# Softplus of a selective scan in two ScalarE operations instead of three

## The chip, the core and the metric

The kernel runs on one core of one Trainium2 chip. The metric is the device time of one execution in microseconds, of which the median of three runs is taken. All data are float32.

## What is computed

Two layers follow each other on an input of 8 images of 64 x 64 places and 192 channels. The first is a Mamba-2 block with depthwise convolutions and a small MLP; the change doesn't touch it. The second is a selective scan (SS2D) in four directions, and its core is this, cut from the reference:

```python
x_dbl = jnp.einsum('bkdl,kcd->bkcl', xs, x_proj_weight)
dts, Bmat, Cmat = ...                       # 12, 16 and 16 rows
dts = jnp.einsum('bkrl,kdr->bkdl', dts, dt_projs_weight)
delta = jax.nn.softplus(dts + dt_projs_bias[None, :, :, None])
A = -jnp.exp(A_logs).reshape(K, D_INNER, D_STATE)      # K = 4, D_INNER = 384, D_STATE = 16
def step(hst, inp):
    d, bm, cm, uu = inp
    dA = jnp.exp(d[..., None] * A[None])
    dBu = (d * uu)[..., None] * bm[:, :, None, :]
    hst = dA * hst + dBu
    y = jnp.einsum('bkdn,bkn->bkd', hst, cm)
    return (hst, y)
```

Softplus is log(1 + exp(v)), here of v = dts + bias, with a bias drawn between -4 and -2.

## The kernel before, in words

The first layer runs for the first 5 ms, then the second layer takes the images one after the other. For each image there is a stage of projections and convolutions (`front`), then the scan (`main`), then normalisation, gate and output projection (`finish`). The `finish` of an image, the `front` of the next and the beginning of its scan (`prologue`, `prologue_of`) share one stage. In that stage a planner, `Flow.run`, writes out the order on each engine: each `step(engine, cost, ...)` carries a cost in microseconds, a change of ScalarE's function table costs 1.3 in its plan, and of all chains' next steps the one that can start first by these costs is put next. The order is then fixed on every engine. A table is loaded where the set changes (`"explog"` for Exp and Ln, `"silu"` for Silu), and once more ahead of `main`. There are nine such stages: the first has no `finish`, the last no `front`, and seven have both.

`main` is written out by hand, and each engine works through its instructions in program order. An image has 32 steps: four directions k, and for each 8 tiles of 512 places. A step has 24 units u = 3 p + d: p counts 8 pairs of states, d counts 3 blocks of 128 channels. One unit does the following.

- DVE runs two scans over 128 x 512 (L1596): `hs` = `ea` x state + `g`.
- POOL copies the last state (`cy`, L1608) and multiplies `hs` by the C row (`hc`, L1610).
- ACT computes `ea` = exp(A delta) for the unit two ahead, two operations (L1569; three buffers), and then two or three `pw` = (delta u) times B (L1554) for units further on. Their numbers are 3, 3 and 2 for d = 0, 1 and 2.
- PE turns `pw` into `g` for the next unit by eight transposes (L1580; two buffers) and then adds `hc` of the unit before into `y` (L1625). For the first direction it also adds a skip term.
- DVE adds a finished `y` into `yacc` after the last p (three times a step, in the last unit and the first two of the next step).

Between the units stand the pieces which prepare the next step, one list for each unit number (`prepare`). Per d they are: `step` (PE, `p_dt`, L1468), `soft` (ACT, three operations, L1475 to L1477), `delta` (DVE, L1482), `times_u` (POOL, `du`, L1489), `turn` (PE, `p_du`, L1495), `keep_du` (DVE, `duT`, L1502), and `repeat_delta` (four DMAs on SP, `dr`, L1536). `p_d`, `p_b`, `p_dt` and `p_du` all share one PSUM bank there, so that each waits until the one before has been read. The list, cut to what matters:

```python
7: [(keep_b,), (step, 0)],
8: [(soft, 0)],
9: [(delta, 0), (step, 1)],
10: [(soft, 1), (times_u, 0)],
11: [(delta, 1), (turn, 0), (repeat_delta, s, 0)],
12: [(keep_du, 0), (step, 2), (times_u, 1)],
13: [(soft, 2)],
14: [(delta, 2), (turn, 1)],
15: [(keep_du, 1), (times_u, 2)],
```

The last step of an image prepares nothing, so 8 x 31 = 248 steps are prepared inside a loop and 8 in the stages between the images.

Of the kernel before, what the change touches and what calls it, by code (L numbers as in the profile page):

```python
# [9 lines left out]
AF = mybir.ActivationFunctionType  # L10
ALU = mybir.AluOpType
# [18 lines left out]
NP1 = N // 2  # L30

EXPLN = "natural_log_exp_and_others"


_P96 = [("cw1", 18), ("cb1", 2), ("l1w", 2), ("l1b", 2), ("cw2", 18), ("cb2", 2), ("l2w", 2), ("l2b", 2), ("fb2", 2)]
# [20 lines left out]
def explog(tc):  # L56

    tc.keep_in_program_order(tc.nc.scalar.preload_act_table_set(EXPLN))

# [31 lines left out]
class Flow:  # L91
# [24 lines left out]
    def pool(self, tag, n):  # L116
        self.slots[tag] = [0.0] * n
# [34 lines left out]
    def run(self):  # L152
        while self.chains:
# [10 lines left out]
            elif req[0] != "wait":  # L164
                engine, weight, do, _, table = req
                if table and table != self.table:
                    self.table = table
                    if table == "explog":
                        self.keep(self.tc.nc.scalar.preload_act_table_set(EXPLN))
                for ins in do() or ():  # L170
# [11 lines left out]
def step(engine, weight, do, after=None, table=None):  # L182
    return engine, weight, do, after, table
# [846 lines left out]
def layer1(tc, consts, x1s, mv1, out, w_in, w_x, w_dt, w_out):  # L1030
    nc = tc.nc
# [6 lines left out]
    with ExitStack() as ctx:  # L1038
        pool = lambda name, bufs, **kw: ctx.enter_context(tc.tile_pool(name=name, bufs=bufs, **kw))
        wp = pool("w1", 1)  # L1040
        sp = pool("s1", 1)
# [49 lines left out]
        o = lambda ins: keeper[-1](ins)  # L1091
# [309 lines left out]
        def scan(xo):  # L1401
# [5 lines left out]
            pools, ready = {}, {}  # L1407
# [12 lines left out]
            def prepare(s, bank=lambda name: mp.tile([128, TT], F32, name=name, tag="mm")):  # L1420
# [3 lines left out]
                st = state[s]  # L1424
# [47 lines left out]

                def soft(d):
                    st["sp", d] = a = pools["pr1"].tile([128, TT], F32, name="spa", tag="tmp")
                    o(nc.scalar.activation(a, st["p_dt", d], AF.Abs))  # L1475
                    o(nc.scalar.activation(a, a, AF.Exp, scale=-1.0))
                    o(nc.scalar.activation(a, a, AF.Ln, bias=1.0))  # L1477

                def delta(d):
                    st["de", d] = pools["pr1"].tile([128, TT], F32, name="de", bufs=3)  # L1480
                    o(
                        nc.vector.scalar_tensor_tensor(  # L1482
                            st["de", d], st["p_dt", d], 0.0, st["sp", d], ALU.max, ALU.add
                        )
                    )

# [13 lines left out]
                def keep_du(d):  # L1500
# [13 lines left out]
                    6: [(turn_b,)],  # L1514
# [9 lines that stand above are left out]
                    16: [(turn, 2)],  # L1524
# [5 lines left out]
            def repeat_delta(s, d):  # L1530

                state[s]["dr", d] = dr = pools["dr1"].tile([128, 2, TT], F32, name="dr")
                de = state[s]["de", d]
                for f in range(2):
                    for i in range(2):
                        o(nc.sync.dma_start(out=dr[i * 64 : i * 64 + 64, f], in_=de[f * 64 : f * 64 + 64]))  # L1536
# [135 lines left out]
            def prologue_of(f, d):  # L1672

                yield "wait", "xd"
                yield "take", "mm"
                yield step("PE", 0.95, lambda: ready["step"](d))
                yield "take", "tmp"
                yield step("ACT", 1.9, lambda: ready["soft"](d), None, "explog")
                r = yield step("DVE", 0.7, lambda: ready["delta"](d))
                f.give("mm", r)  # L1680
                f.give("tmp", r)
                yield step("SP", 0.1, lambda: repeat_delta(0, d), r)
                yield "take", "tmp"
                r = yield step("POOL", 1.3, lambda: ready["times_u"](d), r)
                yield "take", "mm"
                r = yield step("PE", 0.6, lambda: ready["turn"](d))
                f.give("tmp", r)
                yield "wait", "bt"
                r = yield step("DVE", 0.7, lambda: ready["keep_du"](d))
                f.give("mm", r)  # L1690
                f.at["du", d] = r
# [32 lines left out]
            def chains(f, mq, front_pools):  # L1724
                f.pool("tmp", 2)
                return [prologue(f, mq, front_pools)] + [prologue_of(f, d) for d in range(DT)]
# [128 lines left out]
```

## Time and profile before

| what | value |
|---|---|
| median of 3 runs | 24186.39 us (24181.09 to 24191.97) |
| the profiled execution: its time, its span | 24176.65 us, 24174.9 us |
| first layer and first `front`, until the first scan | 5049 us |
| one image's scan loop (second image: 7456.4 to 9620.4) | 2164 us |
| from the last scan of an image to the first of the next | 238 to 240 us |
| ACT ea L1569, pw L1554 | 709 and 601 ns each, 8123.2 and 8875.8 us in all |
| ACT softplus L1475, L1476, L1477 | 575, 630 and 630 ns, 768 of each |
| DVE scan L1596, POOL hc L1610 | 1263 and 2373 ns each |

A profile line names the source line, the engine, the operation, the tile written and those read, the shape and the count; then the busy time, the mean duration, and the time that the engine stood idle just before, with what ended it (`<-`). Back-to-back operations of one engine overlap a little, so the distance from start to start can be smaller than a duration. In a timeline the columns are start, length, engine, line; a bracket gives the idle time before. With 24 units and 31 of 32 steps alike, one step of about 67.6 us (first direction 68.5 us) repeats through the loops.

### The profile page before, as it was taken

What the parts mean: (1) busy time and instruction counts of PE and PEld (TensorE: products, weight loads), DVE (VectorE), ACT (ScalarE), POOL (GpSimd) and SP (SyncE); (2) the same over time, 40 slices, a digit from 0 to 9 for tenths busy, and PEclk for the clock granted to TensorE, in tenths of its full rate; (3) what the DMA queues carried; (4) which work ended last, traced back from release to release, by engine and by line L of the source; (5) the groups of instructions that cost most, each with busy time, mean ns of one, the idle gap of its engine ahead of it and who ended that gap; (6) DMA issues with size and microseconds to landing.
All of it is one profiled execution on the core that took longest, in us unless ns stands there. A gap on an engine that the chain in (4) does not pass through costs nothing.

```text
span 24174.9 us, 313055 instructions
## 1 busy us (share of the span) xinstructions
PE 20986.5 (87%) x100036; PEld 10182.8 (42%) x100036; DVE 21386.3 (88%) x22093; ACT 21415.5 (89%) x38076; POOL 16907.4 (70%) x13639
## 2 busy tenths in 40 slices
PE   7999999978888888888888888888888888888888
PEld 4444444434443444344434443444344434443444
DVE  7888888779998998899889988998899989998998
ACT  5666766679998999899989998999899989998998
POOL 1111111159986998699869986998699779977997
PEclk8999999989999999999999999999999999999999
DMA  2111111122222222222222222222222222222222
GB/s 49 44 44 44 49 44 42 36 86 67 68 66 87 68 67 68 89 66 66 69 87 68 68 68 86 67 68 70 84 68 67 76 78 67 68 75 82 67 67 58
DMA packets 1129702, 1608.05 MB, mean 67 GB/s; under 512 B 259360, under 2 KB 458432, under 8 KB 1118848
## 3 DMA queue, kind: packets, MB, share of 16 engines
q1 hardware_dynamic: 1128064, 1588.03, 23.4%
q8 instruction: 806, 13.21, 0.2%
q14 instruction: 832, 6.82, 0.1%
HBM read 1024.65 MB, written 160.17 MB: 49 GB/s over the span
## 4 chain that ended last, share of the span: by engine, by line
POOL 53%; PE 25%; issue 8%; DVE 6%; ACT 5%; DMA 2%; SPq 1%; POOLq 0%; DVEq 0%; ACTq 0%
POOL hc L1610 47%; POOL cy L1608 4%; PE y L1625 3%; PE p_f L953 3%; DVE xs L1200 3%; PE p_f L973 2%; PE p_x L445 2%; PE g L1580 2%; ACT pw L1554 2%; DMA xc<-xo 2%; PE p_o L870 1%; POOL du L1489 1%; ACT ea L1569 1%; PE p_y L787 1%; PE p_d L1439 1%
## 5 line engine op out<-in xcount | busy, mean ns | idle before, releaser
L1610 POOL TENSOR_TENSOR hc<-hs,cb 128x1024 f32<-128x1024 f32 x6144 | 14577.7, 2373 | 10.3 <-POOL cy L1608 6.7
L1596 DVE TENSOR_TENSOR_SCAN hs<-ea,cy,g 128x512 f32<-128x512 f32 x10752 | 13069.7, 1263 | 783.2 <-PE g L1580 468.3
L1554 ACT ACTIVATE pw<-duT,bt 128x384 f32<-128x384 f32 x16384 | 8875.8, 601 | 11.6 <-DVE duT L1502 11.6
L1625 PE MATMUL y<-hc,sel 128*64 128x512 f32 x24576 | 6658.3, 620 | 2229.1 <-POOL hc L1610 2221.3
L1569 ACT ACTIVATE ea<-dr,an 128x512 f32<-128x512 f32 x12288 | 8123.2, 709 | 159.9 <-DVE hs L1596 131.9
L1580 PEld LDWEIGHTS g<-ident,pw 128*128 128x128 f32 x49152 | 5309.6, 141 | 4320.1 <-issue 2676.5
L1580 PE MATMUL g<-ident,pw 128*128 128x128 f32 x49152 | 6793.2, 280 | 32.4 <-DVE hs L1596 12.9
L1625 PEld LDWEIGHTS y<-hc,sel 128*64 128x64 f32 x24576 | 1229.6, 135 | 3648.1 <-POOL hc L1610 3385.1
L1489 POOL TENSOR_TENSOR du<-de,xc 128x512 f32<-128x512 f32 x768 | 982.9, 1280 | 1632.9 <-DVE de L1482 1618.2
L1608 POOL COPY cy<-hs 128x2 f32<-128x2 f32 x6144 | 1161.7, 189 | 1324.4 <-DVE hs L1596 1211.9
L1596 DVE TENSOR_TENSOR_SCAN hs<-ea,g 128x512 f32<-128x512 f32 x1536 | 1777.0, 1204 | 178.7 <-PE g L1580 138.3
L362 POOL TENSOR_TENSOR s<-xs 96x512 f32<-96x512 f32 x64 | 121.0, 1891 | 2033.2 <-DVE xs L340 1522.3
L1200 DVE SCALAR_TENSOR_TENSOR xs<-pad,p,xs 128x4096 f32<-128x4096 f32 x192 | 860.8, 4484 | 37.6 <-ACT xs L1190 30.4
L1468 PE MATMUL p_dt<-xdbl,wd 13*128 13x512 f32 x1536 | 856.8, 639 | 41.7 <-DVE de L1482 39.7
L362 POOL TENSOR_TENSOR s<-sq 96x512 f32<-96x512 f32 x128 | 210.3, 1643 | 961.7 <-ACT sq L375 890.7
L1439 PE MATMUL p_d<-xc,wx 128*44 128x512 f32 x1536 | 792.2, 598 | 95.0 <-DMA xc<-xo 95.0
L340 DVE SCALAR_TENSOR_TENSOR x<-xx,p,x 96x512 f32<-96x512 f32 x1024 | 784.4, 814 | 19.4 <-ACT x L329 19.4
L953 PE MATMUL p_f<-h,wf 96*128 96x512 f32 x1536 | 764.1, 633 | 24.4 <-ACT zs L547 14.0
L340 DVE SCALAR_TENSOR_TENSOR xs<-xin,p,xs 96x512 f32<-96x512 f32 x1024 | 749.5, 768 | 4.6 <-ACT xs L329 4.6
L1482 DVE SCALAR_TENSOR_TENSOR de<-p_dt,spa 128x512 f32<-128x512 f32 x768 | 524.1, 682 | 254.0 <-ACT spa L1477 253.0
L973 PE MATMUL p_f<-m,wf 128*96 128x512 f32 x1536 | 693.3, 602 | 0.0
L1495 PEld LDWEIGHTS p_du<-ident,du 128*128 128x128 f32 x3072 | 323.1, 141 | 743.2 <-POOL du L1489 500.3
(201 smaller groups left out, 19729.0 us busy)
## 6 DMA issues: line engine op xcount, KB each, us to landing
cb<-cd SPq DMA_DIRECT2D x4096, 128.0 KB
dr<-de SPq DMA_DIRECT2D x3072, 128.0 KB
xc<-xo SPq DMA_DIRECT2D x256, 768.0 KB
e<-csd SPq DMA_DIRECT2D x256, 384.0 KB
xl<-x SPq DMA_DIRECT2D x256, 384.0 KB
xo<-xs SPq DMA_DIRECT2D x48, 1024.0 KB
xo<-xt SPq DMA_DIRECT2D x24, 2048.0 KB
xl<-in_x SPq DMA_DIRECT2D x64, 384.0 KB
```

What stands on the lines that cost most here:

```text
L340: nc.vector.scalar_tensor_tensor(im(out[:, ct]), tap(ct, j), w[:, ct, j : j + 1], im(out[:, ct]), ALU.mult, ALU.add)
L953: nc.tensor.matmul(ps, wf1[:, ct, mt * 128 : mt * 128 + 128], h[:, ct], start=ct == 0, stop=ct == 1)
L973: nc.tensor.matmul(ps[:CP], wf2[:, kt, ct * CP : ct * CP + CP], m[:, kt], start=kt == 0, stop=kt == 5)
L1200: nc.vector.scalar_tensor_tensor(xs, tap(j), kw[:, d, j : j + 1], xs, ALU.mult, ALU.add)
L1489: o(nc.gpsimd.tensor_mul(st["du", d], st["de", d], st["xc"][:, d]))
L1554: nc.scalar.activation(st["pw", p, j][:, :, i], st["duT"][:, j].rearrange("p (g c) -> p g c", c=64), AF.Copy, scale=st["bt"][:, j, n : n + 1],
L1569: nc.scalar.activation(ea[:, f], state[s]["dr", d][:, f], AF.Exp, scale=an[:, k, p, at : at + 1])
L1580: nc.tensor.transpose(g[:, f, j * 128 : j * 128 + 128], state[s]["pw", p, j][:, 2 * d + f].rearrange("p a b -> p (a b)"), ident,)
L1596: nc.vector.tensor_tensor_scan(rev(h[:, f]), rev(ea[:, f]), rev(g[:, f]), 0.0 if first(s) else state[s - 1]["cy"][:, p, d, f : f + 1], ALU ...
L1608: o(nc.gpsimd.tensor_copy(st["cy"][:, p, d], h[:, :, last]))
L1610: o(nc.gpsimd.tensor_mul(hc, h, bc(st["cb", p], 1, [128, 2, TT])))
L1625: o(nc.tensor.matmul(y[half[f]], sel, hc[:, f], start=p == 0 and k > 0, stop=p == NP1 - 1))
```

## The change

`soft` drops the absolute value: ScalarE now computes exp(v) from PSUM, and log(1 + that). `delta` took max(v, 0) and added log(1 + exp(-|v|)); now it takes the minimum of log(1 + exp(v)) and 60 and then the maximum of that and v, so that an overflowing exp can't get through. It is still one `scalar_tensor_tensor` on VectorE, with its two tensors exchanged: the first is now the one in SBUF, the second the one in PSUM. The planner's cost for `soft` in the stages between images goes from 1.9 to 1.3. The counts of all other instructions stay, but for one table load fewer in each of the seven stages that have both `finish` and `front`.

```diff
+BIG = 60.0
...
                 def soft(d):
                     st["sp", d] = a = pools["pr1"].tile([128, TT], F32, name="spa", tag="tmp")
-                    o(nc.scalar.activation(a, st["p_dt", d], AF.Abs))
-                    o(nc.scalar.activation(a, a, AF.Exp, scale=-1.0))
+                    o(nc.scalar.activation(a, st["p_dt", d], AF.Exp))
                     o(nc.scalar.activation(a, a, AF.Ln, bias=1.0))
...
                         nc.vector.scalar_tensor_tensor(
-                            st["de", d], st["p_dt", d], 0.0, st["sp", d], ALU.max, ALU.add
+                            st["de", d], st["sp", d], BIG, st["p_dt", d], ALU.min, ALU.max
                         )
...
-                yield step("ACT", 1.9, lambda: ready["soft"](d), None, "explog")
+                yield step("ACT", 1.3, lambda: ready["soft"](d), None, "explog")
```

In the built program the change of cost moves the order in those seven stages. On ScalarE, after the three softplus and the last `yrs`, the order was: table load, one z, three yacc, ten pw, five z, table load, four ea, table load. It becomes: two yacc, ten pw, one yacc, four ea, table load, six z, table load. On PE the two matmuls of one `p_z` move from ahead of two groups of `p_o` to behind `p_du`. On SP four `dr` transfers come ahead of one `xl` load. On DVE the three deltas come ahead of the three `duT` copies in the first stage (of the first image).

## The prediction

> **What bounds the kernel now.** I read the page first: busy shares, the chain that ended last, the costliest groups.
>
> ```profile
> PE 20986.5 (87%) x100036; PEld 10182.8 (42%) x100036; DVE 21386.3 (88%) x22093; ACT 21415.5 (89%) x38076; POOL 16907.4 (70%) x13639
> ...
> POOL 53%; PE 25%; issue 8%; DVE 6%; ACT 5%; DMA 2%; SPq 1%; POOLq 0%; DVEq 0%; ACTq 0%
> ...
> L1610 POOL TENSOR_TENSOR hc<-hs,cb 128x1024 f32<-128x1024 f32 x6144 | 14577.7, 2373 | 10.3 <-POOL cy L1608 6.7
> ```
>
> Three engines are near 88%, and ScalarE (ACT), the one that the change relieves, is the busiest. But it holds only 5% of the chain; GpSimd (POOL) holds 53%, nearly all in hc. Next I cut the second image's scan loop out, by windows:
>
> ```profile
> 7457.00:9620.00 2163.00, 1865.89 (x10159) 913.88 (x10157) 2017.84 (x1877) 2137.90 (x3848) 2017.87 (x1627) 1.00 0.24 66
> ```
>
> Columns: length, then busy PE, PEld, DVE, ACT, POOL. ACT is busy 98.8% of the loop, POOL and DVE 93.3%. Busy is not bound: the question is who waits for ACT. The page's groups answer it in total, and the lines of the softplus name the waiter:
>
> ```profile
> L1482 DVE SCALAR_TENSOR_TENSOR de<-p_dt,spa 128x512 f32<-128x512 f32 x768 | 524.1, 682 | 254.0 <-ACT spa L1477 253.0
> ```
>
> So VectorE (DVE) lost 253.0 us in front of delta because softplus was late. I sorted the trace's records of L1482 by their place: per step the first delta (piece 9) waits 0, the second (piece 11) 0.51 us on average, the third (piece 14) 0.37. Over the 248 steps that are prepared inside a loop that is 126.5 and 92.9 us; some 33 us are in the eight stages between images. Last, the timeline around one third delta:
>
> ```profile
> 8852.77 2.39 POOL L1610 TENSOR_TENSOR hc<-hs,cb 128x1024 f32<-128x1024 f32 x1
> ...
> 8853.76 1.12 PE L1468 MATMUL p_dt<-xdbl,wd 13*128 13x512 f32 x2
> ...
> 8854.81 1.09 PE L1580 MATMUL g<-ident,pw 128*128 128x128 f32 x8
> 8855.09 1.30 POOL L1489 TENSOR_TENSOR du<-de,xc 128x512 f32<-128x512 f32 x1
> ...
> 8856.04 2.45 DVE L1596 TENSOR_TENSOR_SCAN hs<-ea,cy,g 128x512 f32<-128x512 f32 x2 [0.72 <-ACT pw L1554]
> ...
> 8857.53 0.63 ACT L1476 ACTIVATE spa<-spa 128x512 f32<-128x512 f32 x1
> 8858.19 0.63 ACT L1477 ACTIVATE spa<-spa 128x512 f32<-128x512 f32 x1
> ...
> 8858.86 0.69 DVE L1482 SCALAR_TENSOR_TENSOR de<-p_dt,spa 128x512 f32<-128x512 f32 x1 [0.37 <-ACT spa L1477]
> ...
> 8861.97 0.18 POOL L1608 COPY cy<-hs 128x2 f32<-128x2 f32 x1 [0.67 <-DVE hs L1596]
> ```
>
> The reader is to see three things. POOL has no idle mark until 8861.97, where it waits 0.67 us for the scan behind the delayed delta. The scan at 8856.04 is put down to ACT pw, but PE decides it: a y matmul needs hc, p_dt runs to 8854.88, g to 8855.90, then the scan starts. So of the three softplus of a step only the last is on the path.
>
> **What the Trainium skill says.** "ScalarE: Activation LUTs", What ACT_TABLE_LOAD costs: one element per cycle and lane whatever the function, and back-to-back ACTIVATEs overlap by about 93 ns. The trace agrees: Exp and Ln from SBUF take 630 ns each, Abs from PSUM 575, and pw of 601 ns starts every 507 ns. Same page, Table sets: abs is filler in every set, and natural_log_exp_and_others holds Exp and Ln; so neither removing Abs nor the new pair adds a load inside the loop, where the trace has none. "VectorE: DVE Perf Modes", Why PSUM operands drop a tier: fp32 with a PSUM operand runs at 1x; so delta with its operands exchanged should keep its cost. No run shows that order; I take 691 ns, the median of L1482.
>
> **The change, part by part.**
>
> Removed: 768 Abs. One soft takes 8856.93 to 8858.73 = 1.80 us from its start to the next instruction's. After, Exp reads PSUM (I take Abs's 0.60 from start to start; by the SBUF Exp at most 0.66) and Ln takes 0.54 until the next one starts, so 1.14. ACT is 0.66 us less per softplus, 1.98 per step, 507 us in all. This is the gain only if ACT were the bound.
>
> On the path, in the loop. Third delta: its wait goes, 0.37 per step. What would be late next is the scan before it, ending 8858.49: delta can start about there. The scan after it ends 0.37 earlier, and the 0.67 idle of POOL shrinks to 0.30. p_dt for it was there at 8854.88, ACT would come to it at 8856.93 - 2 x 0.66 = 8855.61, so PE isn't late. The sum over the 248 steps is the 92.9 us above.
>
> Second delta: its 126.5 us go as a wait but are worth nothing, because POOL runs du and hc without a gap from there until the third delta, and PE (y after hc, p_dt, g) sets scan 14. If that cover were gone, they would count: 126.5 is kept as the far end. First delta: 0. The rest of POOL's idle per step (about 4.3 us in all, marked DVE hs) stands where DVE adds yacc, keeps xdbl, or waits for g behind PE's p_dt; ACT has no part in it. ACT's freed time turns into waits for the ea buffers, behind which only pw of later units are queued. No wait is added in the loop.
>
> Delta: the same count on DVE; between -0.05 and +0.05 us each on two of three places gives -25 to +25 us; I take 0.
>
> First image's front: the deltas come 0.66, 1.3 and 1.9 us earlier, and the program now puts all three ahead of the duT copies. du comes earlier, pw at 5043.66 too; I take -3 (0 to -4).
>
> Between images, seven times. The planner's cost 1.9 to 1.3 changes its order; the two built programs show it. Before: yrs, table load, z, yacc x3, pw x10, z x5, load, ea x4, load. After: yrs, yacc x2, pw x10, yacc, ea x4, load, z x6, load. One load (1.283 us by its rows) is saved, but all z go behind ea. z feeds the product, then 24 p_o matmuls, four xl adds, g, and the first scan:
>
> ```profile
> 7440.80 2.38 ACT L1345 ACTIVATE z<-p_z,gb 128x512 f32<-128x512 f32 x4
> ...
> 7442.07 1.76 DVE L1357 TENSOR_TENSOR yacc<-yacc,z 128x1536 f32<-128x1536 f32 x1 [6.38 <-ACT z L1345]
> ...
> 7456.46 1.22 DVE L1596 TENSOR_TENSOR_SCAN hs<-ea,g 128x512 f32<-128x512 f32 x1 [1.31 <-PE g L1580]
> ```
>
> From product to scan it is 14.4 us. After: softplus ends 7427.3 instead of 7429.1; p_z moves behind p_du, so p_du and the last duT come some 1.4 us earlier, pw starts about 7434.3 and runs 5.1, yacc 0.8, ea 2.6, load 1.3: z from 7444.0, its third done at 7445.9, against 7442.07. So +3.8 us each (bounds -1, if p_o's banks hold back nothing and pw comes earlier still, to +7, with nothing gained ahead), +27 in all (-7 to +49). The moved DMAs (four dr ahead of one xl on SP) are hidden: dr is needed by ea at some 7440, all twelve are issued by 7434.8.
>
> Sum: 24176.65 (profiled execution; its span is 24174.9) - 92.9 - 3 + 27 = 24108. That execution is 9.7 us under the runs' median of 24186.39, so on their scale -69 gives 24117.
>
> **Rivals.**
>
> ACT is the bound after all: for it, 98.8% busy; against it, 5% of the chain and POOL's unbroken row. 24186 - 248 x 1.98 - 3 + 27 = 23719. Chance 0.07.
>
> Both late deltas count, and the stage between images costs nothing: 24186 - 92.9 - 126.5 - 3 = 23964; it speaks for it that both waits are real, against it that POOL is full between them. With parts of this, 23970 to 24055. Chance 0.18.
>
> Slower: z behind ea. If the loop's gain is lost because another release (hc after g, as at scan 14) is late at the same moment, and each stage between images costs the full 7 us, it gives 24186 + 49 - 3 = 24232. It decides once the stages cost more than the loop gives: 93 / 7 = 13 us each at full gain, or 3 us each at a gain of about 20. Chance 0.09 for this side in all, of which 0.06 beyond 0.2%.
>
> **How the numbers follow.** Forecast's case 0.66: 24055 to 24180. 0.2% (48 us) is about what a measurement of this kernel can tell from no change: the line is 24138. Of the forecast's case about three quarters lie below it (0.49), the rest is same (0.17); the two faster rivals add 0.25; the slower side gives 0.03 same and 0.06 slower. So faster 0.74, same 0.20, slower 0.06. The range goes from 23965 to 24195: the ACT rival, the slower one's far part and a little of each edge are left out.
>
> **What would show it.** In the changed profile: L1475 to L1477 become two rows of 768; delta's wait for ACT spa falls from 253.0 to under 30; ACT's idle before ea on DVE hs rises by about 1.6 us per step; a step goes from 67.6 to about 67.25; POOL's 0.67 becomes about 0.3; the time from the last scan of an image to the first of the next goes from about 239 to 243. Wrong would be: a step at 65.7 (ACT the bound), at 66.8 (both deltas), or still 67.6, or a delta of over 0.75 us.

## The result and the profile after

The kernel after takes 24087.8 us (median of 5 runs, 24082.19 to 24097.21), the kernel before, with its runs beside these, 24188.55 us (median of 5, 24181.09 to 24194.95). The ratio is 0.996, with a 95% interval of 0.9948 to 0.9971: faster by 0.4%, 101 us. The forecast was 24117 us, 29 us more.

The profiled execution of after took 24097.21 us, with a span of 24095.5 us. Cut at the first and last scan of each image, the two executions differ so:

| part (us) | before | after | difference | predicted |
|---|---|---|---|---|
| until the first softplus of the second layer | 5030.7 | 5044.2 | +13.5 | 0 |
| first softplus to first scan | 18.74 | 14.86 | -3.9 | -3 |
| the eight scan loops | 17317.5 | 17195.8 | -121.7 | -92.9 |
| the seven stages between images | 1670.9 | 1702.2 | +31.3 | +27 |
| after the last scan | 137.0 | 138.4 | +1.4 | 0 |

The first row holds the same instructions in both kernels, so its 13.5 us are a difference between two executions and not an effect of the change; over the twelve profiled executions of this document the row lies between 5013.8 and 5052.2 us. Without it, the change is worth -92.9 us in the profiles (that this is the predicted loop term to the decimal is chance).

First the page of after: the engines, then two groups.

```profile
PE 20932.0 (87%) x100036; PEld 10206.0 (42%) x100036; DVE 21334.2 (89%) x22093; ACT 21051.3 (87%) x37301; POOL 16914.7 (70%) x13639
...
L1598 DVE TENSOR_TENSOR_SCAN hs<-ea,cy,g 128x512 f32<-128x512 f32 x10752 | 13070.0, 1263 | 904.1 <-PE g L1582 662.0
...
L1571 ACT ACTIVATE ea<-dr,an 128x512 f32<-128x512 f32 x12288 | 8140.8, 710 | 432.9 <-DVE hs L1598 367.0
```

The same two groups before:

```profile
L1596 DVE TENSOR_TENSOR_SCAN hs<-ea,cy,g 128x512 f32<-128x512 f32 x10752 | 13069.7, 1263 | 783.2 <-PE g L1580 468.3
...
L1569 ACT ACTIVATE ea<-dr,an 128x512 f32<-128x512 f32 x12288 | 8123.2, 709 | 159.9 <-DVE hs L1596 131.9
```

ACT lost 364 us of busy time, and the span shortened by 79 us. Where the rest went stands in the last columns. ACT waited 159.9 us ahead of `ea` before, and 432.9 now. The scan waited 468.3 us for PE's `g` before, and 662.0 now. So ACT now waits more for others, and part of the gain comes back where the scan waits for PE. The second image's loop, by windows (length, then busy PE, PEld, DVE, ACT, POOL):

```profile
7456.00:9606.00 2150.00, 1857.26 (x10165) 916.95 (x10165) 2012.49 (x1878) 2095.62 (x3755) 2020.28 (x1629) 1.00 0.24 67
```

ACT fell from 98.8% to 97.5% of the loop, POOL and DVE rose from 93.3% to 94.0% and 93.6%. The group of `delta` has lost its wait, as predicted; of 253.0 us for ACT spa 19.0 are left, all outside the loops:

```profile
L1484 DVE SCALAR_TENSOR_TENSOR de<-spa,p_dt 128x512 f32<-128x512 f32 x768 | 508.9, 663 | 20.0 <-ACT spa L1479 19.0 <-DMA out_x<-xl 0.9
```

And the timeline around one third delta, the place that the prediction shows of before:

```profile
8841.64 1.08 PE L1627 MATMUL y<-hc,sel 128*64 128x512 f32 x4 [0.93 <-POOL hc L1612]
...
8842.65 1.12 PE L1471 MATMUL p_dt<-xdbl,wd 13*128 13x512 f32 x2
...
8843.70 1.09 PE L1582 MATMUL g<-ident,pw 128*128 128x128 f32 x8
...
8844.93 2.45 DVE L1598 TENSOR_TENSOR_SCAN hs<-ea,cy,g 128x512 f32<-128x512 f32 x2 [0.95 <-PE g L1582]
8845.09 0.63 ACT L1479 ACTIVATE spa<-spa 128x512 f32<-128x512 f32 x1
...
8847.30 0.66 DVE L1484 SCALAR_TENSOR_TENSOR de<-spa,p_dt 128x512 f32<-128x512 f32 x1
...
8850.38 0.19 POOL L1610 COPY cy<-hs 128x2 f32<-128x2 f32 x1 [0.19 <-DVE hs L1598]
```

Three things are to be seen. The last softplus operation is done at 8845.72, 1.6 us before `delta` starts, so it no longer decides. POOL's wait at the end has gone from 0.67 to 0.19. And at the top stands what the scan waits for instead: `y` waits 0.93 us for `hc` of POOL, `p_dt` and `g` are queued behind it on PE, and the scan waits 0.95 us for `g`. Whether this chain limits the loop, a later experiment asks (PE's pieces ahead of y).

### The profile page after: what moved, and what is told of

Read it like the earlier page. It is cut to its first block, busy times and chain, and to the rows that moved or that the text cites. A ratio compares the mean times of both kernels' runs of the same rounds, so it can differ in the third digit from the quotient of the medians.

```text
span 24095.5 us, 312287 instructions
## 1 busy us (share of the span) xinstructions
PE 20932.0 (87%) x100036; PEld 10206.0 (42%) x100036; DVE 21334.2 (89%) x22093; ACT 21051.3 (87%) x37301; POOL 16914.7 (70%) x13639
## 5 line engine op out<-in xcount | busy, mean ns | idle before, releaser
L1598 DVE TENSOR_TENSOR_SCAN hs<-ea,cy,g 128x512 f32<-128x512 f32 x10752 | 13070.0, 1263 | 904.1 <-PE g L1582 662.0
L1571 ACT ACTIVATE ea<-dr,an 128x512 f32<-128x512 f32 x12288 | 8140.8, 710 | 432.9 <-DVE hs L1598 367.0
L1582 PE MATMUL g<-ident,pw 128*128 128x128 f32 x49152 | 6702.4, 279 | 25.1 <-DVE hs L1598 12.5
L1377 PE MATMUL p_o<-yacc,wo 128*96 128x512 f32 x768 | 417.9, 700 | 205.1 <-DVE yacc L1360 156.7
```

The costliest lines, as they stand in the source:

```text
L1571: nc.scalar.activation(ea[:, f], state[s]["dr", d][:, f], AF.Exp, scale=an[:, k, p, at : at + 1])
L1582: nc.tensor.transpose(g[:, f, j * 128 : j * 128 + 128], state[s]["pw", p, j][:, 2 * d + f].rearrange("p a b -> p (a b)"), ident,)
L1598: nc.vector.tensor_tensor_scan(rev(h[:, f]), rev(ea[:, f]), rev(g[:, f]), 0.0 if first(s) else state[s - 1]["cy"][:, p, d, f : f + 1], ALU ...
```

## The experiments

All ratios are to the kernel before, run on the same chip, with their 95% intervals. The loop figures are from one profiled execution of each; where the loops hold the same instructions, two executions differed by up to 9.3 us in the sum of the eight loops (17195.8 and 17186.5). "Mean of a unit" is taken over the 184 prepared steps of the last three directions, from the start of one unit's scans to that of the next.

### The softplus without the new order

The planner's cost back to 1.9, nothing else, so that the stages between images keep the order of before.

```diff
-                yield step("ACT", 1.3, lambda: ready["soft"](d), None, "explog")
+                yield step("ACT", 1.9, lambda: ready["soft"](d), None, "explog")
```

> The changed softplus with the planner's cost left at 1.9, so that the order between the images is the old one. My theory (the loop gains through the third delta's wait alone, and the seven stages between images lose by z behind ea): loops as in the changed kernel, about 15 us less per image than before; from an image's last scan to the next's first about 237 us instead of 242 to 245; time about 24056. Rival (the stages grew because the loop hands over at another state, not because of the order): the stages stay at about 243 and the time at about 24088.

It took 24058.92 us, ratio 0.9951 (0.9938 to 0.9963). The seven stages take 1673.4 us (before 1670.9, after 1702.2), the loops 17186.5. So the change consists of a gain in the loops and a loss of about 30 us (1702.2 - 1673.4) in the stages, which comes from the order alone. By the medians this version is ahead of the change as it was made; the intervals of the two ratios overlap, so what shows it is the stages.

### The new order without the softplus

The kernel before, with the cost 1.3: the line above alone, the other way round.

> The old three-operation softplus with the planner's cost of 1.3: only the order between the images changes. My theory: loops unchanged; stages between images 243 to 246 us (the 4.5 us of the changed kernel, and up to 2 more as the softplus is longer); time about 24225. Rival (the order costs nothing): 24188.

It took 24213.08 us (21 runs), ratio 1.0014 (1.0008 to 1.0021). The stages take 1715.3 us, +44.4 in all or +6.3 each; the loops (17316.8) and delta's waits in them (126.6 and 94.4 us) are those of before. It agrees with the run before this: the order costs time, and without the shorter softplus ahead of it, it costs more. ACT's timeline in this kernel, at the first such stage, shows how:

```profile
7455.79 2.54 ACT L1569 ACTIVATE ea<-dr,an 128x512 f32<-128x512 f32 x4
...
7459.65 3.58 ACT L1345 ACTIVATE z<-p_z,gb 128x512 f32<-128x512 f32 x6
```

All six `z`, which the output projection and so the next image's first scan wait for, stand behind the four `ea`. Before, one of them was done ahead of the ten `pw` and the rest ahead of `ea`. That the place of `z` is what costs the time is read from this timeline; the order on PE and SP moves along with it, and no run moves `z` alone.

### Only the first softplus, or only the third

The shorter form in the loop for one d alone, the old form elsewhere, cost 1.9. The edit to the kernel before, for the first (for the third, `d == 2`); the part cut off gives `delta` the matching form:

```diff
-                    o(nc.scalar.activation(a, st["p_dt", d], AF.Abs))
-                    o(nc.scalar.activation(a, a, AF.Exp, scale=-1.0))
+                    new = s > 0 and d == 0
+                    if not new:
+                        o(nc.scalar.activation(a, st["p_dt", d], AF.Abs))
+                        o(nc.scalar.activation(a, a, AF.Exp, scale=-1.0))
+                    else:
+                        o(nc.scalar.activation(a, st["p_dt", d], AF.Exp))
...
```

> The two-operation softplus for the first block of channels alone (d = 0, whose delta never waited), in the loop, at the old planner's cost. My theory (ScalarE works in order, so a softplus is late by what all work ahead of it takes; 0.66 us taken out anywhere ahead of the third one is worth its whole wait): second and third delta's waits fall from 126.5 and 92.9 us to near 0 and to under 20; loops 12 to 15 us less per image; time about 24070. Rival (a delta waits for its own softplus' length): loops unchanged, time 24188. Rival (ScalarE is the bound): a third of what ScalarE is spared, 0.66 us x 248 = 164 us less.

> The two-operation softplus for the last block alone (d = 2), in the loop, at the old planner's cost. My theory: the third delta's wait goes, the second's 126.5 us stay and are covered by GpSimd and PE; loops 12 to 15 us less per image; time about 24070, the same as with the first block alone. Rival (both late deltas count): less than the changed kernel, with a rest of about 126 us left over that the full change has and this has not, so slower than it by some 0.5 us per step.

The first alone: 24073.1 us, ratio 0.9957 (0.9944 to 0.9969), loops 17206.0. The third alone: 24064.66 us, ratio 0.9954 (0.9941 to 0.9968), loops 17207.2. The kernel before took 24178.23 us beside these, so they give 105 and 114 us, where all three give 119 (24058.92, the first experiment, of the same series). The groups of `delta` tell how, first with the new form at d = 0 only (the old form's group):

```profile
L1497 DVE SCALAR_TENSOR_TENSOR de<-p_dt,spa 128x512 f32<-128x512 f32 x520 | 348.3, 670 | 38.7 <-ACT spa L1484 33.5 <-DMA cb<-cd 1.1
```

and then with the new form at d = 2 only:

```profile
L1497 DVE SCALAR_TENSOR_TENSOR de<-p_dt,spa 128x512 f32<-128x512 f32 x520 | 353.1, 679 | 159.8 <-ACT spa L1484 159.2
L1491 DVE SCALAR_TENSOR_TENSOR de<-spa,p_dt 128x512 f32<-128x512 f32 x248 | 164.9, 665 | 2.4
```

With the first softplus shortened, both later waits are gone although their softplus are as long as before: ACT's queue as a whole was late by about half a microsecond, and the 0.66 us taken off at the first softplus heal both. With the third alone the second delta still waits 125.2 us in the loops, and the time is the same within the intervals: in the mean of a unit, units 11 and 13 stay at 3.54 and 3.22 us (before 3.55 and 3.25), and unit 14, that of the third delta, falls from 3.40 to 2.96. So the second delta's wait costs next to nothing, as the prediction had it; and of the 1.98 us per step that the change takes from ACT, 0.66 give most of the gain (110.3 or 111.5 us in the loops, against 131.0 with all three).

### One operation more, one operation less

The kernel before with a second `Abs` for d = 0 in the loop, which only takes time:

```diff
                     o(nc.scalar.activation(a, st["p_dt", d], AF.Abs))
+                    if s > 0 and d == 0:
+                        o(nc.scalar.activation(a, st["p_dt", d], AF.Abs))
```

> The kernel before with one Abs more on ScalarE in the loop, ahead of the first softplus of each prepared step (some 0.61 us a step, 151 us in all). My theory (the third delta follows ScalarE's lateness one for one once it waits): its wait goes from 0.37 to some 0.95 us, GpSimd's idle behind it by the same, loops 15 to 19 us longer per image; time 24310 to 24345. Rival (GpSimd and TensorE cover this too, as they cover the second delta): under 24240.

It took 24330.35 us, ratio 1.0061 (1.0048 to 1.0073); the loops 17465.5, +148.0 or 0.60 us per step for an operation of 0.61. Here ACT's work does set the time, one for one, and it does so through the third delta: in the mean of a unit, unit 11 grows by 0.63 us and unit 13 gives 0.74 back, while unit 14 grows by 0.70. The group of `delta` shows the lateness that it puts on all later softplus:

```profile
L1484 DVE SCALAR_TENSOR_TENSOR de<-p_dt,spa 128x512 f32<-128x512 f32 x768 | 524.6, 683 | 578.3 <-ACT spa L1479 577.1
```

In the other direction, the kernel after with cost 1.9 and without the `Ln` in the loop:

```diff
-                    o(nc.scalar.activation(a, a, AF.Ln, bias=1.0))
+                    if s == 0:
+                        o(nc.scalar.activation(a, a, AF.Ln, bias=1.0))
```

> The changed kernel with the old planner's cost, and in the loop with Exp alone in place of Exp and Ln: the logarithm is left out, so that ScalarE has 0.54 us less per softplus, 1.6 us a step, 400 us in all. My theory (ScalarE is off the path once the two-operation form is in): no gain, time about 24059, ScalarE's idle 1.7 to about 3.3 us a step. Rival (ScalarE still bounds the loop in part): up to 400 us less.

It took 24065.02 us, ratio 0.995 (0.9937 to 0.9962), loops 17197.2 against 17186.5 with the `Ln`. What was taken off is more than I had counted (0.54 us per softplus). From the start of a softplus to the start of the operation behind it, it takes 1.14 us in the first experiment and 0.48 here, so 0.66 less and again 1.98 us per step: `Exp` overlaps with the `ea` behind it, and did not with the `Ln`, which reads its result. ACT's idle time per step rose from about 1.7 to about 2.9 us, and nothing came of it. Its loop, by windows:

```profile
7452.80:9600.70 2147.90, 1855.27 (x10164) 916.34 (x10161) 2011.96 (x1878) 2057.39 (x3662) 2017.63 (x1627) 1.00 0.24 67
```

So the kernel before sits at an edge: more work on ACT costs its full length, less pays for about half a microsecond per step and then nothing.

### PE's pieces ahead of y

If the chain `hc`, `y`, `p_dt`, `g`, scan binds now, then `p_dt` and `p_du` should not stand behind a `y` that waits for POOL. In this kernel PE's pieces of a unit are issued between its `g` and its `y`; the list is shifted by a unit where a piece would else come too early; cost 1.9.

```diff
-                    7: [(keep_b,), (step, 0)],
-                    8: [(soft, 0)],
-                    9: [(delta, 0), (step, 1)],
+                    7: [(keep_b,)],
+                    8: [(step, 0), (soft, 0)],
+                    9: [(delta, 0)],
...
+                    early = [x for x in now if x[0].__name__ in ("project", "turn_b", "step", "turn")]
+                    for f, *args in early:
+                        f(*args)
```

> The changed softplus with the old planner's cost, and TensorE's pieces of the next step (project, turn_b, step, turn) put between g and y of a unit, where TensorE waits for hc, instead of behind y; step and turn then come one unit later in the list. My theory (GpSimd is full but for the places where a scan waits for g behind p_dt or p_d): GpSimd's 0.93 us idle behind unit 8 goes or halves, a step is 0.6 to 1.2 us shorter, time 23770 to 23920. Rival (those idle times have another cause, the scans' own extra operations): 24059.

> The same order on TensorE with the old three-operation softplus. My theory (what a shorter softplus is worth depends on who else is late): ScalarE, with 67.2 us of work a step, becomes the bound; a step is 67.2 to 67.5, time 24090 to 24160, so that the two-operation form is worth over 1 us a step here and 0.5 in the order before. Rival (it is worth 0.5 us a step in either order): 120 us over the kernel with this order and the new form.

With the new softplus it took 23832.85 us, ratio 0.9851 (0.9836 to 0.9866), the fastest version that computes everything: 1.5% faster than before, where the change alone gives 0.4%. In the mean of a unit, units 8 and 13 fell from 3.57 and 3.80 us (first experiment) to 2.54 and 2.34, and units 11 and 14 rose from 2.93 and 2.94 to 4.15 and 3.60. With the old softplus and the same order it took 24375.12 us, ratio 1.0077 (1.0065 to 1.009): slower than before, which neither my range (24090 to 24160) nor its rival (120 us over the new form) had. A step took 68.2 us, more than the 67.2 us of work on ACT, from which I had taken the range. The loops of the two, with the new softplus first:

```profile
7433.30:9554.60 2121.30, 1860.31 (x10164) 912.88 (x10162) 2013.18 (x1878) 2081.32 (x3755) 2018.44 (x1627) 1.00 0.24 68
```

```profile
7480.50:9666.60 2186.10, 1882.40 (x10164) 918.94 (x10162) 2010.37 (x1878) 2140.53 (x3848) 2018.22 (x1627) 0.99 0.24 66
```

The difference is 64.8 us per image, 2.1 us per step: in this order the shorter softplus is worth all of its 1.98 us, and 542 us in the medians. Of these, 188 us only undo what the order costs with the old softplus (24375.12 against 24187.44 us of the kernel before beside it). The timeline of the first of the two, around a second delta, shows why:

```profile
8794.71 1.09 PE L1581 MATMUL g<-ident,pw 128*128 128x128 f32 x8
8795.73 1.12 PE L1471 MATMUL p_dt<-xdbl,wd 13*128 13x512 f32 x2
...
8796.78 1.08 PE L1626 MATMUL y<-hc,sel 128*64 128x512 f32 x4
...
8798.48 0.58 ACT L1478 ACTIVATE spa<-p_dt 128x512 f32<-128x512 f32 x1
...
8799.75 0.69 DVE L1484 SCALAR_TENSOR_TENSOR de<-spa,p_dt 128x512 f32<-128x512 f32 x1 [1.00 <-ACT spa L1479]
```

`p_dt` follows `g` at once and is there at 8796.85; ACT comes to it at 8798.48 only, and `delta` waits 1.00 us for it. PE's chain is out of the way, and ACT is late again. The groups of `delta` of this kernel show it in total, 280.2 us of it at the second and 144.6 at the third:

```profile
L1484 DVE SCALAR_TENSOR_TENSOR de<-spa,p_dt 128x512 f32<-128x512 f32 x768 | 522.5, 680 | 444.4 <-ACT spa L1479 443.8 <-DMA out_x<-xl 0.5
```

With the old softplus in the same order:

```profile
L1485 DVE SCALAR_TENSOR_TENSOR de<-p_dt,spa 128x512 f32<-128x512 f32 x768 | 530.9, 691 | 953.3 <-ACT spa L1480 952.2 <-DMA cb<-cd 1.1
```

### The deltas later

If those waits are what is left, `delta` one or two units later should remove them. The edit to the kernel of the last section:

```diff
-                    11: [(delta, 1), (repeat_delta, s, 0)],
-                    12: [(turn, 0), (keep_du, 0), (times_u, 1)],
-                    13: [(step, 2), (soft, 2)],
-                    14: [(delta, 2)],
-                    15: [(turn, 1), (keep_du, 1), (times_u, 2)],
-                    17: [(turn, 2), (keep_du, 2)],
+                    11: [(repeat_delta, s, 0)],
+                    12: [(delta, 1)],
+                    13: [(turn, 0), (keep_du, 0), (times_u, 1)],
+                    14: [(step, 2), (soft, 2)],
+                    16: [(delta, 2)],
+                    17: [(turn, 1), (keep_du, 1), (times_u, 2)],
+                    19: [(turn, 2), (keep_du, 2)],
```

> TensorE's pieces ahead of y as in the run before, and the second and third delta one and two units later in the list (12 and 16), with what follows them (turn and keep_du at 13, 17 and 19, the third step and soft at 14). There, delta waited 1.13 and 0.58 us a step for ScalarE. My theory (a delta that comes later than its softplus can be waits for nothing): both waits under 0.1 us, a step 65.2 to 65.8 us instead of 66.03, time 23640 to 23780. Rival (ScalarE, with 65.3 us of work a step, bounds the loop now, or GpSimd covered these waits): within 40 us of 23833.

> The same list with Exp alone in the loop: the logarithm is left out, 1.6 us less on ScalarE a step. If ScalarE bounds the kernel with the late deltas, this gains up to 400 us more; if GpSimd and TensorE do, nothing beyond 40 us.

With this list and the `Ln` it took 23977.44 us, ratio 0.9911 (0.9898 to 0.9925): slower than with the deltas early, and outside both my range and the rival's. The waits of `delta` for ACT did go:

```profile
L1484 DVE SCALAR_TENSOR_TENSOR de<-spa,p_dt 128x512 f32<-128x512 f32 x768 | 510.2, 664 | 19.6 <-ACT spa L1479 18.6 <-DMA out_x<-xl 0.9
```

They came back elsewhere. What DVE waited for between 7500 and 9500 us (total, number, longest), with the deltas early and then late:

```profile
DVE de L1484 <- ACT spa L1479: 50.8, 60, 1.3
DVE hs L1597 <- PE g L1581: 23.1, 62, 1.6
DVE duT L1504 <- PE p_du L1497: 16.0, 31, 0.9
```

```profile
DVE hs L1598 <- PE g L1582: 50.9, 92, 1.8
DVE duT L1504 <- PE p_du L1497: 27.5, 56, 1.0
DVE hs L1598 <- ACT ea L1571: 15.4, 24, 0.8
```

The 50.8 us have become waits for `g`, for `ea`, for `p_du` and, not shown, for `pw`; with these and the smaller ones DVE's waits rose from 93.1 to 110.5 us. So this list isn't free; `delta` was not moved alone in it, and a later `delta` by itself was not tried. Without the `Ln` in the loop, the last kernel took 23587.07 us, ratio 0.9751 (0.9738 to 0.9764): its step is 65.04 us instead of 66.55. That is 1.5 us for the 1.98 taken off ACT (counted as 1.6 ahead of the run, as above). So in this order ACT's work sets most of the time, though no `delta` in the loop waits for it. The second image's loop, first with the `Ln`, then without:

```profile
7435.60:9572.90 2137.30, 1875.36 (x10164) 919.36 (x10162) 2011.47 (x1878) 2084.53 (x3755) 2018.00 (x1627) 1.00 0.24 67
```

```profile
7382.30:9472.50 2090.20, 1839.79 (x10164) 914.49 (x10162) 2009.66 (x1878) 2030.83 (x3662) 2012.58 (x1627) 1.00 0.25 69
```

ACT's busy time falls by 53.7 us and the loop by 47.1, so ACT stays at 97 to 98% of it. Why the late order is 0.52 us per step slower than the early one, with the same work on ACT, stays open. POOL stands idle 1.1 us per step in units 16 and 17 of the late order (in the early order not at all there), which is gone without the `Ln`; that the third softplus now comes ahead of other `pw` may be the reason, but it was not moved alone.

## Why the prediction was right, step by step

- **The bound.** "Busy is not bound" held: ACT freed 1.98 us per step, and a step got shorter by 0.49 (121.7 us over 248 prepared steps). In the last three directions it went from 67.63 to 67.18 us in the mean, forecast 67.25. The rival with ACT as the bound (a step at 65.7) is out. The Trainium skill, "Perfetto Trace Analysis", Identifying the Most-Contended Engine, takes the engine of highest occupancy for the one to optimize first; here that engine, at 98.8% of the loop, gave only its lateness. But the extra `Abs` shows that the opposite, "ACT isn't the bound", would have been wrong too: it bound up to 0.5 us and no further.
- **Third delta, -92.9 us: right in cause, too small.** Its 92.9 us are gone, but the loops gave 121.7. Units 11 to 14 of a step took 3.55, 2.93, 3.25 and 3.40 us in the mean, and now 2.93, 2.93, 3.85 and 2.94; no other unit moves by more than 0.03 us. Unit 14 gave 0.46, of which 0.37 is the wait. The other 0.09 come from `delta` itself, which now follows a busy DVE: in the timeline of after it starts at 8847.30, ahead of the preceding scan's end at 8847.38, and is some 0.03 shorter. I had priced `delta` at one value for both cases.
- **Second delta, worth nothing: right.** Unit 11 gave 0.62 and unit 13 took 0.60 back; the sum over units 11 to 13 is -0.02. "No wait is added in the loop" was wrong, since the wait for `g` grew, but it grew only by what it had covered. The scan at 8844.93, with its 0.95 us for `g` behind `y` and `p_dt`, is where it came back, as named. The run with the third softplus alone shows the same from the other side. So the rival in which both deltas count is out.
- **Delta's cost, 0: right for the exchange, not for the state.** From before to after, the median went from 691 to 661 ns. Sorted by whether DVE stood idle ahead of it (by more than 0.15 us), `delta` takes 692 ns in the mean with such a wait and 667 without in the kernel before, and 687 and 662 in the kernel after. So the wait makes 25 ns, and the new form, with its operands exchanged and other operations, 5 ns, some 4 us over all 768.
- **First front, -3: measured -3.9.**
- **Stages between images, +27: measured +31.3**, +4.5 each against +3.8. Its parts, in the first of the seven: from the first softplus to `pw` 10.33 us instead of 12.07, so 1.7 earlier (estimated 1.4); to the product of `yacc` and `z` 21.83 instead of 18.41, so +3.4; and a part that I had left out, from the product to the first scan 16.17 instead of 14.39, so +1.8 (14.75 to 16.42 over the seven, +1.4 in the mean). What precedes the softplus is some 0.7 shorter (0.4 in the mean). A view of ACT in this stage of after has a longer stop at the sixth `z`, 1.56 us where it was 0.41 before: PE had not yet made its input. That this stop makes the +1.8 was not tested.

```profile
7433.96 2.54 ACT L1571 ACTIVATE ea<-dr,an 128x512 f32<-128x512 f32 x4
7436.52 1.28 ACT L1348 ACT_TABLE_LOAD   x1
7437.82 3.00 ACT L1348 ACTIVATE z<-p_z,gb 128x512 f32<-128x512 f32 x5
...
7442.38 0.69 ACT L1348 ACTIVATE z<-p_z,gb 128x512 f32<-128x512 f32 x1 [1.56 <-PE p_z L1330]
```

- **The table load.** One less per stage, 1.28 us by this row, as taken; the Trainium skill's 1283 ns ("ScalarE: Activation LUTs", What ACT_TABLE_LOAD costs) agrees. The drain of about 1380 ns that it adds to each switch doesn't show in this view: `z` starts 1.30 us after the load did. The order that saved the load cost more than the load.
- **ACT's idle time, +1.6 per step: shown +1.0, and the reading was too simple.** The idle column rose from 0.84 to 1.84. But from the start of a `pw` to the start of the `ea` behind it, the mean went from 535 to 600 ns, about 21 times per step: 21 x 0.065 = 1.4 us. Neighbours overlap by some 95 ns, and a wait shows as idle only beyond that.

## What to carry to other kernels

A wait for a nearly full engine shows how late its queue is. Where nothing else covers that wait, as at the third delta, this lateness is what a cheaper operation wins; where something covers it, as at the second, it wins nothing. So ask what stands right behind: here GpSimd and the queue of TensorE were half a microsecond away, and once TensorE's pieces were moved, the same edit was worth four times as much per step (2.1 against 0.5 us), partly because that order is slower than the old one without it. If a planner's cost is part of an edit, look at its order by itself: here it gave back about a quarter of what the edit won.

## What was unexpected of the hardware

The same `scalar_tensor_tensor` over 128 x 512 takes 667 ns right behind another operation of VectorE and 692 ns when it starts after waiting (kernel before); in the kernel whose deltas all wait but one (the old softplus with PE's pieces first) the mean is 691. The Trainium skill, "VectorE: DVE Perf Modes", The TRN2 errata, gives 691 ns for an fp32 `tensor_tensor` of 512 elements, which agrees with the waiting case of this related operation; that section doesn't tell the two apart. An operation of ScalarE that reads the result of the one before starts about 32 ns after its end, while independent neighbours overlap by about 95 ns: that is why leaving out a `Ln` of 630 ns freed 0.66 us. And the time until the first softplus, with the same instructions, took 13.5 us longer in one profiled execution than in the other.
